# Fewer SBUF operands on VectorE, pinned scaling and builds, and heads contracted in pairs in a two-layer Fourier attention kernel

## The chip, the cores and the metric

One Trainium2 core (float32 throughout). The metric is device time in microseconds (us) of one launch. Lower is better. The kernel before took 567.58, 564.03 and 561.96 us in three runs, median 564.03.

## The reference, cut to what matters

Two layers are applied to x of shape (2, 56, 128, 128): x = x + layer(groupnorm(x)). K, Q, V, P, M0 and M1 are spectral convolutions that keep 32 x 16 modes, each with a 1x1 skip. Below, A = 8 heads.

```python
q, k, v = fno_layer(xa, ...)                 # 1 -> 8 heads for each of 56 channels
scores = einsum('baks,bals->bakl', qh, kh) / sqrt(H * W)
attn = softmax(scores, axis=-1)              # 56 x 56 for each head
out = einsum('bakl,bals->baks', attn, vh)
out = fno_layer(out, Pw, ...)                # 8 heads -> 1
att = inorm(out + xa, gan, ban)
an = inorm(att, g2, b2)
h = fno_layer(an, M0w, ..., norm=True, act=True)      # gelu
h = fno_layer(h, M1w, ..., norm=True)
y = inorm(h, gmo, bmo) + att
```

## The kernel before, in words

The picture is held whole in SBUF (`X2`), and attention is done in the space of modes, where a batch has 56 channels by 32 x 16 complex modes. Each of two layers L works through both batches b. The stages of a batch, with their names in the code, are:

- `turn` (layer 0) or `end` (layer 1) transposes rows on PE (L361) and takes the statistics.
- `modes_chain` finishes the group norm (L454 to L464: tiny operations on 128x1 or 128x2 tiles), scales the plane (L475), transforms it over both axes (L479, L484, L497) to the modes `xf`.
- `gram` and `gram_chain` make the channel matrix (L507, L525) and its norms (`vd` L532).
- `scale_x` multiplies the picture in place by the norm's scale, eight pieces of 120x1024 (L546).
- `scores` (L572, L591), `values` (L613), `softmax_chain` (L630 to L649), `mix_chain` (L657 to L674) and `heads` (L685) are the attention. `AT` is the transposed attention matrix, `MI` the head mixing matrix, `D` the result of `heads`.
- `norms_chain` (L698 to L739) does P, both instance norms and the first inverse transform (`inverse`, L397 and L402).
- `gelu` (L747 to L831) synthesises the picture strip by strip, `h_chain` (L845 to L890) prepares the last one, and `end` (L936, L939) adds everything. In layer 0 POOL's L939 also writes the next layer's picture, which L361 then transposes.

POOL builds the weight matrices `WU`, `WT` and `WM` (`build` L337, `build_m` L344), four instructions each for WU and WT in every layer.

Two things set the order. `_woven(lead, bulk)` traces the steps of a chain of small operations between pieces of bulk work. A scheduler then reorders what it may and writes one list for each engine, and every engine runs its list in order. `tc.keep_in_program_order(i)` forbids the scheduler to move `i` ahead of the instruction traced before it on its engine. PSUM is handed out from two pools: `bank()` has two buffers of one bank, `pair()` three of two banks. An instruction that needs a buffer waits for the last reader of the one it gets.

Of the kernel before, what the change touches and what calls it, by code (L numbers as in the profile page):

```python
# [166 lines left out]
def fno_layers(ctx: ExitStack, tc: tile.TileContext, x, out, weights, small, const):  # L167
# [239 lines left out]
    def multiply(n, src, dst):  # L407
# [12 lines left out]
        S.copy(dst.rearrange("p (h m) -> p h m", h=2), p[:, :, :224])  # L420
# [93 lines left out]
    def gram_chain(L, b, st):  # L514
        xf, p = st["xf"], st["gram"]
        nm = little(f"nm{b}", [1, K])
        V.tensor_scalar(nm, xf[0:1, :K], -float(N * N), None, ALU.mult)
# [14 lines left out]
        V.scalar_tensor_tensor(vd, gc[:, :K], 1.0 / (N * N), ident[:K, :K], ALU.mult, ALU.mult)  # L532
# [21 lines left out]
    def room(b):  # L554
# [7 lines left out]
    def scores(L, b, st):
# [3 lines left out]
        G.tensor_tensor(MI[:K], _bc(ident[:K, :K], 1, HEADS), _bc(d["mix"][:K], 2, K), ALU.mult)  # L566
# [59 lines left out]
    def softmax_chain(L, b, st):  # L626
# [3 lines left out]
        V.tensor_tensor(SC, grid(sc[:, :224], 4), _bc(rl, 1, 4), ALU.mult)  # L630
        top, tot = little(f"top{b}", [N, 4]), little(f"tot{b}", [N, 4])
        V.tensor_reduce(top, SC, AX.X, ALU.max)
        V.tensor_tensor(SC, SC, _bc(top, 2, K), ALU.subtract)
        S.activation(SC, SC, AF.Exp, scale=rk)
        V.tensor_reduce(tot, SC, AX.X, ALU.add)
        V.reciprocal(tot, tot)
        V.tensor_tensor(SC, SC, _bc(tot, 2, K), ALU.mult)
        yield 4.5

        p = pair()  # L640
        for a in range(4):
            for c in range(2):
                for r in range(2):
                    T.matmul(
                        p[64 * r : 64 * r + 64, c, K * a : K * a + K], lhsT=R["SC"][64 * c : 64 * c + K, a, :],
                        rhs=ident[64 * c : 64 * c + K, 64 * c : 64 * c + K], start=True, stop=True,
                        tile_position=(64 * c, 64 * r), skip_group_check=True,
                    )
# [28 lines left out]
    def heads(L, b, st):  # L677
        R = room(b)
        AT, VT = grid(R["AT"]), R["VT"].rearrange("p t (e m) -> p t e m", e=2)
        p = pair()  # L680
        for t in range(4):
            for a in range(HEADS):
                for e in range(2):
                    for c in range(2):
                        T.matmul(  # L685
                            p[64 * e : 64 * e + 64, c, K * t : K * t + K],
                            lhsT=VT[64 * c : 64 * c + K, t, e, 64 * a : 64 * a + 64],
                            rhs=AT[64 * c : 64 * c + K, a, :], start=(a == 0), stop=(a == 7),
                            tile_position=(64 * c, 64 * e), skip_group_check=True,
                        )  # L690
# [4 lines left out]
    def norms_chain(L, b, st):
        (par, d), D, R, pb = prs[L], st["D"], P[b], st["pb"]
        Pm, u, y0, sqy, s1, s2 = (R[:, 448 * j : 448 * j + 448] for j in range(6))
        V.tensor_tensor(Pm, pb[:, :448], D, ALU.add)  # L698
        yield 1.6
        multiply(0, grid(Pm), y0)  # L700
        S.activation(sqy, y0, AF.Square)
        V.scalar_tensor_tensor(u, Pm, 2.0, D, ALU.mult, ALU.subtract)
        V.tensor_tensor(u, u, D, ALU.mult)
# [12 lines left out]
        V.scalar_tensor_tensor(k3[:, 2:3], k3[:, 1:2], EPS, tm, ALU.mult, ALU.add)  # L716
# [7 lines left out]
        v1, v2 = grid(s1), grid(s2)  # L724
# [115 lines left out]
    def h_chain(L, b, st):  # L840
# [7 lines left out]
        V.scalar_tensor_tensor(mv[:, 1:2], mv[:, 0:1], mv[:, 0:1], mv[:, 1:2], ALU.mult, ALU.add)  # L848
# [114 lines left out]
    build(WUv, tcs, 0, range(0, 8, 2))  # L963
# [82 lines left out]
```

## Time and profile before

| | before |
|---|---|
| runs, us | 567.58, 564.03, 561.96 (median 564.03) |
| profiled execution, us | 563.96, of which the span is 562.0 |
| PE (matmul) busy | 465.8 us, 83% of the span |
| DVE (VectorE) busy | 341.3 us, 61% |
| ACT (ScalarE) busy | 191.0 us, 34% |
| POOL (GpSimd) busy | 175.2 us, 31% |
| mean granted TensorE clock | 0.895 of 2.4 GHz |

The span runs from the first to the last instruction. What lies outside it is 1.96 us. A float32 matmul of the program shows as two matmul records in the trace, so x128 there are 64 matmuls of the program. The orders of instructions below count matmuls of the program.

### The profile page before, as it was taken

What the parts mean: (1) busy time and instruction counts of PE and PEld (TensorE: products, weight loads), DVE (VectorE), ACT (ScalarE), POOL (GpSimd) and SP (SyncE); (2) the same over time, 40 slices, a digit from 0 to 9 for tenths busy, and PEclk for the clock granted to TensorE, in tenths of its full rate; (3) what the DMA queues carried; (4) which work ended last, traced back from release to release, by engine and by line L of the source; (5) the groups of instructions that cost most, each with busy time, mean ns of one, the idle gap of its engine ahead of it and who ended that gap; (6) DMA issues with size and microseconds to landing.
All of it is one profiled execution on the core that took longest, in us unless ns stands there. A gap on an engine that the chain in (4) does not pass through costs nothing.

```text
span 562.0 us, 15794 instructions
## 1 busy us (share of the span) xinstructions
PE 465.8 (83%) x7176; PEld 317.9 (57%) x7176; DVE 341.3 (61%) x568; ACT 191.0 (34%) x238; POOL 175.2 (31%) x201
## 2 busy tenths in 40 slices
PE   2347998789989999979659859989989999886695
PEld 2323867659766576636444446958857555543431
DVE  1565387941426885677867977920344874767475
ACT  2432240151437436514213313151546456402000
POOL 2394517991000000055546841910000000055300
PEclk9998896986999998988759969996999998988599
DMA  8991001030000000017443210010000000027434
GB/s 187 240 213 22 2 2 41 6 81 27 3 3 3 1 1 2 1 31 213 150 146 100 69 50 5 7 52 3 3 2 3 1 1 2 1 65 232 132 121 141
DMA packets 13170, 33.29 MB, mean 59 GB/s; under 512 B 2080, under 2 KB 2848, under 8 KB 13088
## 3 DMA queue, kind: packets, MB, share of 16 engines
q1 hardware_dynamic: 12960, 32.23, 21.6%
q8 instruction: 56, 0.92, 0.7%
q10 hardware_dynamic: 144, 0.07, 0.1%
q14 instruction: 10, 0.08, 0.0%
HBM read 21.02 MB, written 11.01 MB: 57 GB/s over the span
## 4 chain that ended last, share of the span: by engine, by line
PE 53%; DVE 21%; ACT 8%; issue 7%; POOL 5%; DMA 5%; DVEq 0%; SPq 0%; POOLq 0%; ACTq 0%
PE pair L762 7%; PE pair L747 6%; PE pair L811 4%; PE pair L591 4%; PE bank L507 4%; PE pair L685 4%; DMA X<-x 3%; PE bank L572 3%; POOL X L939 3%; PE bank L799 2%; DVE WT L402 2%; PE bank L382 2%; PE bank L437 2%; PE bank L327 2%; PE bank L674 2%
## 5 line engine op out<-in xcount | busy, mean ns | idle before, releaser
L369 DVE BATCH_NORM_STATS2 stats<-P 128x6 f32<-128x448 f32 x64 | 35.9, 611 | 43.9 <-ACT P L364 31.9
L831 DVE BATCH_NORM_STATS2 stats<-P 128x6 f32<-128x512 f32 x64 | 40.6, 681 | 18.7 <-ACT P L829 18.6
L546 DVE TENSOR_TENSOR X<-X,gvr 120x1024 f32<-120x1024 f32 x32 | 50.7, 1609 | 0.0
L939 POOL TENSOR_TENSOR X<-P,xr 128x1024 f32<-128x1024 f32 x16 | 38.6, 2427 | 27.6 <-DVE P L936 18.1
L936 DVE SCALAR_TENSOR_TENSOR P<-P,hs,pair 128x1024 f32<-128x1024 f32 x32 | 39.9, 1270 | 11.3 <-PE pair L762 11.0
L829 ACT ACTIVATE P<-pair 128x1024 f32<-128x1024 f32 x32 | 32.6, 1026 | 30.8 <-PE pair L762 30.2
L811 PEld LDWEIGHTS pair<-C,P 120*128 120x128 f32 x256 | 27.7, 147 | 20.6 <-issue 11.5
L747 PE MATMUL pair<-C,WT 32*128 32x128 f32 x512 | 28.3, 325 | 11.8 <-DVE P L936 6.3
L762 PE MATMUL pair<-X,Be 57*64 57x512 f32 x256 | 38.0, 694 | 0.0
L762 PE MATMUL pair<-X,Bs 57*64 57x512 f32 x256 | 37.7, 630 | 0.0
L337 POOL TENSOR_TENSOR WT<-tc,C 128x1024 f32<-128x1024 f32 x8 | 30.0, 3778 | 22.6 <-ACT tc L331 14.6
L507 PE MATMUL bank<-P 128*64 128x56 f32 (+1 forms) x1024 | 36.6, 236 | 0.0
L591 PEld LDWEIGHTS pair<-xf,WU 64*64 64x64 f32 x1024 | 32.8, 136 | 6.5 <-issue 5.7
L811 PE MATMUL pair<-C,P 120*128 120x120 f32 x256 | 35.6, 282 | 0.7 <-ACT P L829 0.5
L747 PEld LDWEIGHTS pair<-C,WT 32*128 32x128 f32 x512 | 23.2, 218 | 22.5 <-issue 8.2
L591 PE MATMUL pair<-xf,WU 64*64 64x56 f32 x1024 | 35.7, 221 | 0.0
L507 PEld LDWEIGHTS bank<-P 128*64 128x64 f32 (+1 forms) x1024 | 34.9, 150 | 0.9 <-issue 0.5
L361 PE MATMUL pair<-C,X 120*128 120x120 f32 x128 | 20.7, 316 | 17.1 <-POOL X L939 17.0
L812 ACT COPY WT<-pair 128x896 f32<-128x896 f32 x32 | 28.9, 906 | 14.3 <-PE pair L811 14.0
L367 ACT COPY P<-pair 128x896 f32<-128x896 f32 x16 | 14.5, 904 | 56.5 <-PE pair L361 56.5
L391 POOL MEMSET WT<- 128x256 f32 x4 | 1.3, 313 | 101.8 <-PE bank L799 68.0
L361 PEld LDWEIGHTS pair<-C,X 120*128 120x128 f32 x128 | 16.5, 167 | 27.7 <-POOL X L939 21.8
(237 smaller groups left out, 877.1 us busy)
## 6 DMA issues: line engine op xcount, KB each, us to landing
X<-x SPq DMA_DIRECT2D x16, 448.0 KB
xr<-x SPq DMA_DIRECT2D x32, 224.0 KB
out<-P SPq DMA_DIRECT2D x32, 224.0 KB
store<-X SPq DMA_DIRECT2D x16, 224.0 KB
xr<-store SPq DMA_DIRECT2D x16, 224.0 KB
stage<-weights SPq DMA_DIRECT2D x2, 544.0 KB
C<-const_all SPq DMA_DIRECT2D x1, 621.0 KB
X<-x SPq DMA_DIRECT2D x2, 256.0 KB
```

The lines of the kernel that those rows point to most:

```text
L361: T.transpose(p[:, s, N * e : N * e + 120], X2[:120, b, i, :], ident[:120, :120])
L369: V.bn_stats(stats[:, 2 * g + s, :], dst[:, 448 * s : 448 * s + 448])
L507: T.matmul(p[u : u + m, :K], lhsT=P[b][:, K * i : K * i + m], rhs=plane[b][:, i, :], start=(i < 2), stop=(i == N - 1), tile_position=(0, u ...
L546: V.tensor_tensor(v, v, _bc(st["gvr"][:120], 1, 8), ALU.mult)
L591: T.matmul(p[64 * e : 64 * e + 64, k, K * a : K * a + K], lhsT=WUv[64 * e : 64 * e + 64, t + k, a, :], rhs=xv[64 * e : 64 * e + 64, t + k, ...
L747: T.matmul(both[j // 2][:, j % 2, N * e : N * e + N], lhsT=Z[32 * j : 32 * j + 32, o : o + N], rhs=C["gw"][32 * j : 32 * j + 32, :], start ...
L762: T.matmul(p[64 * c : 64 * c + 64, r, :], lhsT=Bs[q, :], rhs=X2[q, b, s : s + 4, :].rearrange("p e w -> p (e w)"), start=False, stop=stop, ...
L811: T.transpose(p[:, r, N * e : N * e + 120], h3[:120, o : o + N], ident[:120, :120])
L829: S.activation(h3, both[v].rearrange("p r m -> p (r m)"), AF.Gelu)
L831: V.bn_stats(stats[:, 4 * A + 2 * v + r, :], h3[:, 512 * r : 512 * r + 512])
L936: V.scalar_tensor_tensor(h3, h3, st["hs"], both[v].rearrange("p r m -> p (r m)"), ALU.mult, ALU.add)
L939: G.tensor_tensor(dst, h3, xr[:, n % 3, :], ALU.add)
```

## The change

- **Operands.** VectorE operations on small tiles that read two SBUF tensors become `tensor_scalar` with a column as scalar (L460, L455, L872 and others), or read one operand from PSUM (softmax works on the scores' bank, `multiply` returns its bank, and a `t` in a bank takes one product of L725 and L883). `nm` (L517) and the scaling L885 go to ACT.
- **Heads.** `AT` and `MI` are stored with two heads on the two halves of the partitions, so `mix` takes 4 matmuls in place of 8, the transposes of `AT` 8 in place of 16, and `heads` 64 matmuls of 128 rows in place of 128 of 56. `values` lays out its result to fit: 32 matmuls of 256 columns for 16 of 512.
- **Order.** `scale_x`, `build` and `build_m` are pinned. In the passage to layer 1 the WU builds are traced between the strips of `end` of batch 1. In the diff `G` is POOL, `V` DVE, `S` ACT, `T` PE.

```diff
@@ build
-            G.tensor_tensor(
+            tc.keep_in_program_order(G.tensor_tensor(
...
+            yield
@@ multiply
-        S.copy(dst.rearrange("p (h m) -> p h m", h=2), p[:, :, :224])
+        return p[:, :, :224]
@@ modes_chain
-        V.scalar_tensor_tensor(mv[:, 1:2], mv[:, 0:1], mv[:, 0:1], mv[:, 1:2], ALU.mult, ALU.add)
+        V.tensor_scalar(mv[:, 1:2], mv[:, 0:1], mv[:, 0:1], mv[:, 1:2], ALU.mult, ALU.add)
...
-        V.tensor_tensor(gv, gs[:, 0:1], gs[:, 0:1], ALU.mult)
-        V.tensor_tensor(gv, gs[:, 1:2], gv, ALU.subtract)
-        S.activation(gv, gv, AF.Sqrt, bias=eps)
+        V.tensor_scalar(gv, gs[:, 0:1], gs[:, 0:1], gs[:, 1:2], ALU.mult, ALU.subtract)
+        S.activation(gv, gv, AF.Sqrt, bias=eps, scale=-1.0)
...
-        V.scalar_tensor_tensor(sh, gs[:, 0:1], -1.0, gv, ALU.mult, ALU.mult)
+        V.tensor_scalar(sh, gs[:, 0:1], gv, -1.0, ALU.mult, ALU.mult)
@@ gram_chain
-        V.scalar_tensor_tensor(vd, gc[:, :K], 1.0 / (N * N), ident[:K, :K], ALU.mult, ALU.mult)
+        V.scalar_tensor_tensor(vd, p[:K, :K], 1.0 / (N * N), ident[:K, :K], ALU.mult, ALU.mult)
@@ scale_x
-            V.tensor_tensor(v, v, _bc(st["gvr"][:120], 1, 8), ALU.mult)
+            tc.keep_in_program_order(V.tensor_tensor(v, v, _bc(st["gvr"][:120], 1, 8), ALU.mult))
@@ softmax_chain
-        V.tensor_tensor(SC, grid(sc[:, :224], 4), _bc(rl, 1, 4), ALU.mult)
+        z = grid(sc[:, :224], 4)
+        V.tensor_tensor(z, z, _bc(rl, 1, 4), ALU.mult)
...
-        V.tensor_tensor(SC, SC, _bc(tot, 2, K), ALU.mult)
+        V.tensor_tensor(SC, z, _bc(tot, 2, K), ALU.mult)
@@ heads
-        for t in range(4):
-            for a in range(HEADS):
+        p = bank()
+        for t in range(8):
+            for a in range(4):
                 for e in range(2):
-                    for c in range(2):
-                        T.matmul(
...
+                    T.matmul(
+                        p[64 * e : 64 * e + 64, K * t : K * t + K], lhsT=VT[:, t // 2, e, t % 2, a, :], rhs=AT[:, a, :],
+                        start=(a == 0), stop=(a == 3), tile_position=(0, 64 * e), skip_group_check=True,
+                    )
@@ norms_chain
-        multiply(0, grid(Pm), y0)
-        S.activation(sqy, y0, AF.Square)
...
+        p = multiply(0, grid(Pm))
+        S.activation(halves(sqy), p, AF.Square)
+        V.tensor_copy(halves(y0), p)
...
-        V.tensor_tensor(v1, grid(D), _bc(rows[:, 0, :], 1, 8), ALU.mult)
-        V.tensor_tensor(v2, grid(y0), _bc(rows[:, 1, :], 1, 8), ALU.mult)
-        V.tensor_tensor(s1, s1, s2, ALU.add)
+        t = bank()[:, :448]
+        V.tensor_tensor(grid(t), grid(y0), _bc(rows[:, 1, :], 1, 8), ALU.mult)
+        V.tensor_tensor(grid(s1), grid(D), _bc(rows[:, 0, :], 1, 8), ALU.mult)
+        V.tensor_tensor(s1, s1, t, ALU.add)
@@ h_chain, one line of nine
-        V.tensor_tensor(w_, w_, d["m12"][:K], ALU.mult)
-        V.tensor_tensor(u_, u_, w_, ALU.subtract)
+        V.tensor_scalar(u_, w_, d["m12"][:K], u_, ALU.mult, ALU.subtract)
@@ the passage to layer 1
+            last = end(0, 1, s1, stats[1])
+            next(last)
...
-            build(WUv, tcs, 0, range(0, 8, 2))
-            _run(_woven(modes_chain(1, 0, stats[0], st[1][0]), end(0, 1, s1, stats[1])))
+            _run(_woven(
+                modes_chain(1, 0, stats[0], st[1][0]), _with(last, build(WUv, tcs, 0, range(0, 8, 2))),
+            ))
```

The line numbers of the changed kernel are 2 to 7 higher: L546 becomes L550, L630 L638, L725 and its neighbours L731 to L733, L939 L946, while L337 stays.

First place: DVE in layer 0, before the softmax of batch 0 (L630). `rr` and `vd` belong to `gram_chain`; the tile with the lower number is that of batch 0. Before:

```order
L532 SCALAR_TENSOR_TENSOR vd_843<-gc_840,C 56x56
L546 TENSOR_TENSOR X_86<-X_86,gvr_760 120x1024
L533 TENSOR_REDUCE vc_844<-vd_843 56x1
L546 TENSOR_TENSOR X_86<-X_86,gvr_760 120x1024 x2
L540 RECIPROCAL rr_914<-rr_914 128x57
L546 TENSOR_TENSOR X_86<-X_86,gvr_760 120x1024
L528 COPY gc_994<-bank 56x56
L546 TENSOR_TENSOR X_86<-X_86,gvr_760 120x1024
L532 SCALAR_TENSOR_TENSOR vd_997<-gc_994,C 56x56
L546 TENSOR_TENSOR X_86<-X_86,gvr_760 120x1024
L533 TENSOR_REDUCE vc_998<-vd_997 56x1
L546 TENSOR_TENSOR X_86<-X_86,gvr_760 120x1024
```

In the changed kernel:

```order
L536 SCALAR_TENSOR_TENSOR vd_841<-bank,C 56x56
L537 TENSOR_REDUCE vc_842<-vd_841 56x1
L544 RECIPROCAL rr_912<-rr_912 128x57
L550 TENSOR_TENSOR X_86<-X_86,gvr_553 120x1024
L532 COPY gc_993<-bank 56x56
L536 SCALAR_TENSOR_TENSOR vd_996<-bank,C 56x56
L537 TENSOR_REDUCE vc_997<-vd_996 56x1
L550 TENSOR_TENSOR X_86<-X_86,gvr_553 120x1024 x3
L544 RECIPROCAL rr_1078<-rr_1078 128x57
L550 TENSOR_TENSOR X_86<-X_86,gvr_553 120x1024 x4
L638 TENSOR_TENSOR bank<-bank,rr_912 128x224
L640 TENSOR_REDUCE top_1192<-bank 128x4
```

The scalings between the `vd` lines were those of batch 1 (gvr_760), with batch 0's ahead of the place. They are now batch 0's own, behind its `vd`, and the softmax of batch 0 stands behind all eight. Batch 1's eight stand later, in `norms_chain` of batch 0.

Second place: POOL in the passage from layer 0 to 1. X_86 is the next layer's picture; P_113 is batch 0 and P_114 batch 1. Before:

```order
L939 TENSOR_TENSOR X_86<-P_113,xr 128x1024 x3
L337 TENSOR_TENSOR WU<-tc_1191,C 128x1024 x2
L939 TENSOR_TENSOR X_86<-P_113,xr 128x1024
L566 TENSOR_TENSOR P_113<-C,der_1136 56x448
L337 TENSOR_TENSOR WU<-tc_1191,C 128x1024
L487 COPY P_113<-gv_2969 128x128
L489 TENSOR_SCALAR P_113<-sh_2970 128x1 x2
L939 TENSOR_TENSOR X_86<-P_114,xr 128x1024 x6
L337 TENSOR_TENSOR WT<-tc_1191,C 128x1024 x2
L939 TENSOR_TENSOR X_86<-P_114,xr 128x1024 x2
```

In the changed kernel:

```order
L946 TENSOR_TENSOR X_86<-P_113,xr 128x1024 x4
L572 TENSOR_TENSOR P_113<-C,der_1135 64x224 x2
L491 COPY P_113<-gv_2869 128x128
L493 TENSOR_SCALAR P_113<-sh_2870 128x1 x2
L946 TENSOR_TENSOR X_86<-P_114,xr 128x1024
L337 TENSOR_TENSOR WU<-tc_1190,C 128x1024
L946 TENSOR_TENSOR X_86<-P_114,xr 128x1024
L337 TENSOR_TENSOR WU<-tc_1190,C 128x1024 x2
L946 TENSOR_TENSOR X_86<-P_114,xr 128x1024
L337 TENSOR_TENSOR WU<-tc_1190,C 128x1024
L946 TENSOR_TENSOR X_86<-P_114,xr 128x1024 x3
L337 TENSOR_TENSOR WT<-tc_1190,C 128x1024 x2
```

The WU builds left the adds of batch 0 and stand between those of batch 1. Two WT builds stay ahead of the last two adds of batch 1, which follow the last row.

Third place: DVE in layer 1, where the norms of batch 0 and the softmax of batch 1 meet. P_113 is batch 0's room, P_114 batch 1's. Before:

```order
L725 TENSOR_TENSOR P_113<-D_4002,bank 128x448
L726 TENSOR_TENSOR P_113<-P_113,bank 128x448
L729 TENSOR_TENSOR dc_4066<-bm_4065,bank 1x56
L727 TENSOR_TENSOR P_113<-P_113 128x448
L445 TENSOR_TENSOR Bs_4264<-BTx_3892,bank 128x56
L728 TENSOR_SCALAR P_113<-P_113,C 128x56
L630 TENSOR_TENSOR P_114<-bank,rr_3726 128x4x56
L730 TENSOR_SCALAR P_113<-dc_4066,der_1136 1x56
L632 TENSOR_REDUCE top_4237<-P_114 128x4
```

In the changed kernel:

```order
L550 TENSOR_TENSOR X_86<-X_86,gvr_3320 120x1024 x3
L638 TENSOR_TENSOR bank<-bank,rr_3607 128x224
L640 TENSOR_REDUCE top_4060<-bank 128x4
L641 TENSOR_TENSOR bank<-bank,top_4060 128x224
L643 TENSOR_REDUCE tot_4061<-bank 128x4
L644 RECIPROCAL tot_4061<-tot_4061 128x4
L645 TENSOR_TENSOR P_114<-bank,tot_4061 128x4x56
L731 TENSOR_TENSOR bank<-P_113,bank 128x448
L732 TENSOR_TENSOR P_113<-D_3823,bank 128x448
```

The whole softmax of batch 1, with its bank, now stands ahead of the first product of batch 0's norms, which needs a bank of its own for `t`. Before, the products came first. Layer 0 has the same order.

## Rows read from the trace of the kernel before

**Rows 1.** The page: busy time of the engines (engine, us, share, instructions).

```profile
PE 465.8 (83%) x7176; PEld 317.9 (57%) x7176; DVE 341.3 (61%) x568; ACT 191.0 (34%) x238; POOL 175.2 (31%) x201
```

**Rows 2.** Windows: busy us (count) of PE, PEld, DVE, ACT, POOL; clock, DMA, GB/s.

```profile
90.00:100.00 10.00, 10.00 (x127) 8.37 (x124) 7.47 (x5) 0.18 (x1) 10.00 (x5) 0.54 0.19 57
140.00:240.00 100.00, 96.45 (x1485) 64.92 (x1481) 59.72 (x138) 52.91 (x65) 4.17 (x7) 0.98 0.01 2
...
380.00:390.00 10.00, 9.35 (x202) 8.93 (x206) 0.61 (x3) 0.81 (x3) 0.31 (x1) 0.62 0.01 3
```

**Rows 3.** Waits of PE: line, what it waited for: total us, times, longest.

```profile
PE pair L361 <- POOL X L939: 17.0, 3, 9.4
...
PE bank L479 <- DVE P L475: 8.2, 4, 6.9
...
PE bank L536 <- DVE vd L532: 4.0, 1, 4.0
PE pair L613 <- POOL WT L337: 1.4, 1, 1.4
```

**Rows 4.** Timeline of DVE, 29 to 36 us: start, duration, instruction.

```profile
29.31 3.85 DVE L460 TENSOR_TENSOR gv<-gs 128x1 f32<-128x1 f32 x1
...
34.60 1.60 DVE L475 TENSOR_SCALAR P<-P,gv,sh 128x1792 f32<-128x1792 f32 x1
```

**Rows 5.** Timeline of POOL beside it.

```profile
28.81 0.93 POOL L566 TENSOR_TENSOR P<-C,der 56x448 f32<-56x448 f32 x1
...
33.22 1.33 POOL L273 TENSOR_TENSOR stage<-stage 128x544 f32<-128x544 f32 x1
```

**Rows 6.** Timeline of DVE, `h_chain` of batch 1, both layers.

```profile
262.04 0.14 DVE L867 TENSOR_SCALAR f<-c 56x1 f32<-56x1 f32 x1
...
262.64 2.32 DVE L872 TENSOR_TENSOR f<-f,der 56x1 f32<-56x1 f32 x1
...
279.61 2.03 DVE L885 TENSOR_SCALAR WU<-WU,C 128x56 f32<-128x56 f32 x1
...
509.88 1.87 DVE L858 TENSOR_TENSOR WU<-WU,xf 128x448 f32<-128x448 f32 x1
...
517.49 1.90 DVE L878 TENSOR_TENSOR f<-f,r 56x1 f32<-56x1 f32 x1
```

**Rows 7.** Timeline of POOL beside the first of them.

```profile
261.53 1.06 POOL L344 TENSOR_TENSOR WM<-tc,C 128x512 f32<-128x512 f32 x1
```

**Rows 8.** Lines L546 and L337: count, duration ns minimum/median/maximum, first and last start.

```profile
L546 DVE TENSOR_TENSOR X<-X,gvr x32: 1149/1207/4123, 79.3 to 362.4; 120x1024 f32<-120x1024 f32 x32
...
L337 POOL TENSOR_TENSOR WU<-tc,C x8: 1942/1952/1964, 57.8 to 289.2; 128x1024 f32<-128x1024 f32 x8
L337 POOL TENSOR_TENSOR WT<-tc,C x8: 1944/2922/11702, 87.7 to 353.7; 128x1024 f32<-128x1024 f32 x8
```

**Rows 9.** Timeline of POOL, end of layer 0.

```profile
281.55 2.34 POOL L939 TENSOR_TENSOR X<-P,xr 128x1024 f32<-128x1024 f32 x1
...
317.32 5.82 POOL L337 TENSOR_TENSOR WT<-tc,C 128x1024 f32<-128x1024 f32 x2
327.76 5.66 POOL L939 TENSOR_TENSOR X<-P,xr 128x1024 f32<-128x1024 f32 x2 [4.62 <-DVE P L936]
```

**Rows 10.** Timeline of PE: half of `heads` twice, half of a `gram`.

```profile
103.30 2.07 PE L507 MATMUL bank<-P 128*64 128x56 f32 x64
...
389.05 3.68 PE L685 MATMUL pair<-P 56*64 56x56 f32 x128
...
422.54 2.09 PE L685 MATMUL pair<-P 56*64 56x56 f32 x128
```

**Rows 11.** Timeline of DVE, the third place of the change.

```profile
405.40 0.62 DVE L725 TENSOR_TENSOR P<-D,bank 128x448 f32<-128x448 f32 x1 [3.60 <-PE bank L432]
...
407.61 0.39 DVE L630 TENSOR_TENSOR P<-bank,rr 128x224 f32<-128x224 f32 x1
```

**Rows 12.** Timeline of ACT there.

```profile
405.92 1.28 ACT L634 ACT_TABLE_LOAD   x1
```

More of the change, by code (lines that the diff above doesn't have):

```diff
@@ L405, in inverse, with multiply @@
             )
-    def multiply(n, src, dst):
+    def multiply(n, src):
         p = pair()
@@ L516, in gram_chain @@
         nm = little(f"nm{b}", [1, K])
[L517 removed]
+        S.activation(nm, xf[0:1, :K], AF.Copy, scale=-float(N * N))
         T.matmul(
@@ L565, in scores @@
         G.tensor_tensor(SG[:K], _bc(ident[:K, :K], 1, HEADS), _bc(d["score_g"][:K], 2, K), ALU.mult)
-        G.tensor_tensor(MI[:K], _bc(ident[:K, :K], 1, HEADS), _bc(d["mix"][:K], 2, K), ALU.mult)
+        for c in range(2):
+            q = slice(64 * c, 64 * c + 64)
+            G.tensor_tensor(MI[q], _bc(C["fold"][q, :K], 1, 4), _bc(d["mix"][q, 4 * c : 4 * c + 4], 2, K), ALU.mult)
         G.memset(R["SC"][:, :, K:], 0.0)
@@ L636, in softmax_chain @@
+        V.tensor_tensor(z, z, _bc(top, 2, K), ALU.subtract)
+        S.activation(z, z, AF.Exp, scale=rk)
+        V.tensor_reduce(tot, z, AX.X, ALU.add)
         V.reciprocal(tot, tot)
-        V.tensor_tensor(SC, SC, _bc(tot, 2, K), ALU.mult)
+        V.tensor_tensor(SC, z, _bc(tot, 2, K), ALU.mult)
         yield 4.5
-        p = pair()
+        p = bank()
         for a in range(4):
             for c in range(2):
[L643 to L648, printed above, removed]
@@ L649, in softmax_chain @@
-        S.activation(R["AT"].rearrange("p (c m) -> p c m", c=2), p[:, :, :224], AF.Copy, scale=rk)
-        yield 1.0
+                q = slice(64 * c, 64 * c + K)
+                T.matmul(
+                    p[64 * c : 64 * c + 64, K * a : K * a + K], lhsT=R["SC"][q, a, :], rhs=ident[q, q], start=True, stop=True,
+                    tile_position=(64 * c, 64 * c), skip_group_check=True,
+                )
+        S.activation(R["AT"], p[:, :224], AF.Copy, scale=rk)
+        yield 0.8
     def mix_chain(L, b, st):
@@ L659, in mix_chain @@
+        T.matmul(p[:K, :K], lhsT=ident[:, :K], rhs=ident[:, :K], start=False, stop=True)
         BT = little(f"BT{b}", [K, 64])
@@ L715, in norms_chain @@
         V.tensor_scalar(tm, p[:K, 1:2], d["A02"][:K], None, ALU.mult)
-        V.scalar_tensor_tensor(k3[:, 2:3], k3[:, 1:2], EPS, tm, ALU.mult, ALU.add)
+        V.tensor_scalar(k3[:, 2:3], k3[:, 1:2], EPS, tm, ALU.mult, ALU.add)
         S.activation(k3, k3, AF.Sqrt)
@@ L847, in h_chain @@
         V.bn_aggr(mv, st["stats"].rearrange("p n s -> p (n s)"))
-        V.scalar_tensor_tensor(mv[:, 1:2], mv[:, 0:1], mv[:, 0:1], mv[:, 1:2], ALU.mult, ALU.add)
+        V.tensor_scalar(mv[:, 1:2], mv[:, 0:1], mv[:, 0:1], mv[:, 1:2], ALU.mult, ALU.add)
         V.tensor_scalar(mv, mv, 0.5, None, ALU.mult)
@@ L855, in h_chain @@
         y1, s1, s2 = (fb[:, 448 * j : 448 * j + 448] for j in range(3))
-        multiply(1, grid(hm), y1)
-        S.activation(s1, y1, AF.Square)
-        V.tensor_tensor(s2, y1, hm, ALU.mult)
+        p = multiply(1, grid(hm))
+        S.activation(halves(s1), p, AF.Square)
+        V.tensor_tensor(halves(s2), p, halves(hm), ALU.mult)
+        S.copy(halves(y1), p)
         yield 1.6
@@ L882, in h_chain @@
         rows = spread(*dg)
-        V.tensor_tensor(grid(s2), grid(y1), _bc(rows[:, 0, :], 1, 8), ALU.mult)
-        V.tensor_tensor(s1, s2, D, ALU.add)
-        V.tensor_scalar(s1[:, :K], s1[:, :K], C["syn"], None, ALU.mult)
+        t = bank()[:, :448]
+        V.tensor_tensor(grid(t), grid(y1), _bc(rows[:, 0, :], 1, 8), ALU.mult)
+        V.tensor_tensor(s1, t, D, ALU.add)
+        S.activation(s1[:, :K], s1[:, :K], AF.Copy, scale=C["syn"])
         V.tensor_tensor(s1[0:1, :K], st["dcq"], rows[0:1, 1, :], ALU.subtract)
@@ L962, in fno_layers @@
     ))
-    build(WUv, tcs, 0, range(0, 8, 2))
+    _run(build(WUv, tcs, 0, range(0, 8, 2)))
     for L in range(2):
@@ L967, in fno_layers @@
         _run(_woven(chain(modes_chain(L, 1, stats[1], s1), more), gram(0, s0)))
-        build(WTv, tcs, 16, range(0, 8, 2))
-        build_m(tcs)
+        _run(chain(build(WTv, tcs, 16, range(0, 8, 2)), build_m(tcs)))
         if L == 0:
```

78 lines of the change are left out of this document (36 added, 42 removed).

## The prediction

> **What bounds the kernel now.** Read the busy shares first: PE works 83% of the span and DVE 61% [rows 1]. PE is the bound, but not everywhere, so I split the span into stretches. In 140 to 240 us PE works 96.45 of 100 us at a clock of 0.98 [rows 2]; nothing that helps DVE, ACT or POOL is worth anything there. In other stretches PE stands still, and behind a pause the granted clock sits near its lower level of 1.2 GHz: 0.54 in 90 to 100 and 0.62 in 380 to 390 [rows 2]. A matmul then costs almost twice as much: the same half of `heads` takes 2.09 us or 3.68 [rows 10]. A gap so costs more than its length.
>
> PE's list of waits gives the gaps names: 17.0 us for L939, POOL's adds at the end of layer 0 (9.4 in one), 8.2 for L475, 4.0 for `vd` L532, 1.4 for a WT build [rows 3]. The timelines of DVE and POOL tell why those are late. L460 works on 128 numbers and takes 3.85 us at 29.31 [rows 4], while POOL runs instruction after instruction from 28.81 on; L460 ends at 33.16, and POOL's next long one, L273, starts at 33.22 [rows 5]. In `h_chain` L872 takes 2.32 and L878 1.90, both with two SBUF operands on 56 numbers, where L867 takes 0.14 [rows 6]. POOL is hurt as well: a WU build always takes 1.95, a WT build, which runs beside the scalings L546, up to 11.7 for its time, and a scaling up to 4.12 around a median of 1.21 [rows 8]. **DVE operations with two SBUF operands and POOL hold each other up**, and PE waits behind both.
>
> The Trainium skill, in "SBUF — State Buffer", section "Who interferes with whom", says that a VectorE instruction with two SBUF inputs blocks against a GpSimd instruction that reads SBUF, until the first of the two is done. By that L460 would have waited only for L566, up to 29.74, some 0.4 us; it waited through seven instructions, so the trace is harsher than the page, and the first term below would by the page be 0.4.
>
> **The change, part by part** (+ is time saved, against the profiled execution of 563.96 us, 0.07 below the median; 1.96 of it lies outside the span and stays).
>
> (a) Group norm of batch 0, layer 0. L460 and L461 become one operation with a column as scalar, so up to 3.85 - 0.16 = 3.7 us go. But L475 is next: it took 1.60 at 34.60 while POOL ran [rows 4], and if it now starts inside POOL's run it may be held to the gap at 33.2 [rows 5]. That starts it 1.4 earlier than 34.60. I take **+1.6**; bounds 0.4 and 4.
>
> (b) 66 to 100 us. The early `values` that waited 1.4 for a WT build [rows 3] now stand later, as WT is traced behind. The stretch behind that wait ran at 0.54, so 10 us hold 5.4 of full speed [rows 2], and 4.6 were lost. I take 1.4 and half of 4.6: **+3.5**; bounds 0 (another wait sends the clock down) and 6.
>
> (c) Scalings. They leave the place ahead of `vd`, so PE's 4.0 wait for it [rows 3] goes. In exchange all eight of batch 0, 8 x 1.21 = 9.7 us [rows 8], stand ahead of its softmax, which delays it a little: I take 1.2. Net 2.8 in layer 0, and 1 in layer 1, where no such wait is listed: **+3.8**; bounds -1 and 6.
>
> (d) Two heads at once. `heads` goes from 128 matmuls to 64, but the old ones use four quarters of the array and the new ones two halves. 64 old ones take 2.09, 33 ns each; L507 has the new form (128 rows, two column halves, 56 columns), and 32 of those take 2.07, 65 ns each [rows 10]. So 128 x 33 = 4.2 becomes 64 x 65 = 4.1: nothing. What is left is 8 fewer transposes at 33 and 4 fewer mix matmuls at 65, half a microsecond, four times: **+2**; bounds 0 and 4.
>
> (e) Norms of batch 0 beside the softmax of batch 1. Now the products start at 405.40 and the softmax at 407.61 [rows 11]. In the new order the whole softmax stands first, since `t` wants a bank. It can't start before the scores end, at 407.6. Its six short DVE and ACT operations of 0.39 [rows 11] make 2.4, and the load of ACT's table, 1.28 and so far hidden behind a wait [rows 12], now waits for DVE and joins the chain: the products start at about 411.3, 6 us late. PE's list has the transposes of AT, the inverse and then `values` in that order, so PE can't run past. Two pinned scalings of 1.21 also precede the transposes L402. Some 0.5 is won back, as part of the scores is earlier: 5.5, and 1 for more time at the low clock. Twice: **-13**; bounds -6 and -22.
>
> (f) End of layer 0. From 283.9, when batch 0's last add ends, to the last of batch 1, 333.4, is 49.5 us [rows 9]. POOL's work in it will be eight adds of 2.34 [rows 9], four WU and two WT builds of 1.95 [rows 8]: 30.4, since no scaling runs beside it; and batch 0's last add comes up to 3.9 earlier, two WU builds being gone from ahead of it. What PE can get is its 17.0 of waiting [rows 3]. DVE's and DMA's part stays, and two WT builds still stand ahead of the last adds (2 x 1.95 in place of 5.82 [rows 9]). I take **+13**, `h_chain`'s gains in layer 0 included; bounds 4 (the two WU builds alone) and 18 (with the clock).
>
> (g) `h_chain` of batch 1, layer 1. L878 loses 1.75 and L858 1.2 [rows 6]; the pieces that read `multiply` and `t` from PSUM about 1 more: **+4**; bounds 1 and 5. Elsewhere the same edits lie under PE's work [rows 2] and count nothing; if PE were not full there, each would give some tenths.
>
> Sum: 1.6 + 3.5 + 3.8 + 2 - 13 + 13 + 4 = 14.9, so 563.96 - 14.9 = **549 us**.
>
> **The rivals.**
>
> *Slower: the scalings sit in the softmax's way.* Batch 1's eight pinned scalings (9.7 us, [rows 8]) all stand in DVE's list inside the norms of batch 0. I hid all but 2.4 of them in waits. If they don't fit, inverse, AT and mix come up to 9.7 later per layer, PE pauses, and `heads` of batch 1 runs at 3.68 per half instead of 2.09, 3.2 more [rows 10]. That is 6.5 + 9.7 + 3.2 = 19.4 per layer, 38.8 in place of 13: 575 us. It decides for slower when (e) costs over 33.5. For it: the clock did fall after such a pause at 380 [rows 2]. Against it: DVE has an idle 3.60 just there, ahead of L725 [rows 11]. Chance 0.13.
>
> *No change: the stall only changes its owner.* A `tensor_scalar` may be held by POOL too. For it: L885 took 2.03 on 128x56 with one tensor operand in SBUF [rows 6]. Against it: L867, a `tensor_scalar` on 56 numbers, took 0.14 while POOL's L344 ran from 261.53 to 262.59 [rows 6, 7]. Then (a) is 0.4, (b) and (c) 1 each, (g) 0.5, and (f) 9: 0.4 + 1 + 1 + 2 - 13 + 9 + 0.5 = 0.9, or 563 us. Chance 0.15. The Trainium skill, same page and section, says that `tensor_scalar` can enter a mode that takes the port shared with GpSimd, which is this rival's rule; L885 agrees, L867 doesn't.
>
> *More: (e) costs nothing,* because PE has batch 0's synthesis to do meanwhile. Against it: in PE's list just six of those matmuls stand ahead of the mix of batch 1. Then 549 - 13 = 536 us. Chance 0.11.
>
> *More: two heads at once do halve `heads`.* If 128 rows cost 33 ns like 56 rows, 2 us go four times: 541 us. L507 speaks against it [rows 10]. Chance 0.06.
>
> **How the numbers follow.** The forecast has 0.55, with a range of its own of 541 to 558 from the bounds; 549 is its middle. The range goes from the third rival to the second, 536 to 564, and leaves out the first. One per cent, 5.6 us, is what can be told from no change here. Faster by more: 0.52 of the forecast, 0.17 of the third and fourth, 0.02 of the second: 0.71. Within: 0.03 and 0.13 of the forecast and the second, 0.16. Slower: 0.13, the first.
>
> **What will show it.** (a) gv's operation takes 0.16, and L479's wait at 36 shrinks by less than 2. (c) no wait for `vd`; scalings behind it with a median near 1.2 and no maximum over 2. (d) half of the new `heads` takes 2.1 at full clock, not 1.05. (e) a wait for the inverse's input, and the ACT table load between two steps of softmax 1. (f) WT builds of about 2, L361's 9.4 gone, adds of batch 1 done 31 to 40 us after those of batch 0. (g) L878's successor at 0.15. I am wrong if (e) is hidden or doubled, or if L361 still waits for POOL: those two terms are the largest and of opposite sign.

## The result and the profile after

The changed kernel took 553.75 us (median of four runs) against 563.8: a ratio of 0.967, 95% interval 0.956 to 0.978. A second series gave 556.03 against 565.1, 0.983 (0.978 to 0.988). Both lie in the forecast range, 5 to 7 us above the forecast of 549. Its runs spread from 543.28 us at a mean granted clock of 0.927 to 561.92 at 0.896. The ratios here and below leave out, for both kernels, the runs that took over 1.5% longer than the fastest of the same kernel in the same series, so they differ from the quotient of the medians (553.75/563.8 = 0.982). The profiled execution, 547.76 us with a span of 546.0, is one of the shorter ones.

The busy shares of the changed kernel, to be held against [rows 1]: PE is busy 7 us less, DVE 23, POOL 17.

```profile
PE 458.8 (84%) x6696; PEld 315.0 (58%) x6696; DVE 318.6 (58%) x556; ACT 190.3 (35%) x242; POOL 158.5 (29%) x205
```

PE's waits, against [rows 3]. The waits of L540 for `vd` (L536) and of the early `values` for a WT build no longer appear:

```profile
PE pair L363 <- POOL X L946: 13.4, 10, 3.0
...
PE bank L652 <- DVE Bs L450: 10.6, 2, 5.3
...
PE bank L483 <- DVE P L479: 2.4, 3, 2.0
```

The 9.4 us wait for one add is gone, the wait for the scaled plane shrank from 8.2 to 2.4, and 10.6 us of a new wait came. The scalings and the WT builds, against [rows 8]: no scaling takes over 2.1, and every WT build takes 1.95.

```profile
L550 DVE TENSOR_TENSOR X<-X,gvr x32: 1160/1214/2052, 93.4 to 390.9; 120x1024 f32<-120x1024 f32 x32
...
L337 POOL TENSOR_TENSOR WT<-tc,C x8: 1944/1950/1955, 81.2 to 333.8; 128x1024 f32<-128x1024 f32 x8
```

Time follows best by landmarks, here the starts and ends of groups on PE's timeline, in us of the span. "+ t" is the changed kernel with one edit, told below, in its second trace.

| landmark | before | changed | its 2nd trace | two heads alone | two heads + pin | changed + t |
|---|---|---|---|---|---|---|
| layer 0: first gram | 57.4 | 51.9 | 56.0 | 52.4 | 52.3 | 55.2 |
| last gram ends | 105.4 | 94.6 | 98.5 | 100.1 | 99.8 | 97.3 |
| heads 0, start to end | 125.3-136.4 | 111.5-119.2 | 115.6-123.1 | 119.2-126.2 | 114.5-126.6 | 114.4-126.9 |
| heads 1 starts | 161.7 | 150.6 | 154.4 | 150.4 | 153.7 | 153.8 |
| inverse of batch 1 | 185.6 | 178.8 | 182.6 | 174.4 | 177.7 | 178.5 |
| layer 1: first transposition | 250.0 | 242.8 | 249.1 | 241.5 | 241.7 | 242.8 |
| last transposition | 335.5 | 315.8 | 322.5 | 324.1 | 319.0 | 317.2 |
| heads 0, start to end | 381.5-392.7 | 361.7-368.8 | 368.7-375.7 | 368.6-377.0 | 364.8-371.9 | 363.1-370.2 |
| heads 1 starts | 418.0 | 400.1 | 407.1 | 401.2 | 397.1 | 395.5 |
| inverse of batch 1 | 441.9 | 428.3 | 435.2 | 428.0 | 421.1 | 420.2 |
| last matmul ends | 555.9 | 539.9 | 547.0 | 541.2 | 532.9 | 531.4 |

The changed kernel's lead over before runs 5.5, 10.8, 17.2, 11.1, 6.8, 7.2, 19.7, 23.9, 17.9, 13.6, 16.0. It falls twice by 10 us, in the same place of both layers, and what the passage to layer 1 wins, 12.5, comes in one piece.

### The profile page after: what moved, and what is told of

The parts are those of the page before. It is cut to its first block, busy times and chain, and to the rows that moved or that the text cites. A ratio compares the mean times of both kernels' runs of the same rounds, so it can differ in the third digit from the quotient of the medians.

```text
span 546.0 us, 14842 instructions
## 1 busy us (share of the span) xinstructions
PE 458.8 (84%) x6696; PEld 315.0 (58%) x6696; DVE 318.6 (58%) x556; ACT 190.3 (35%) x242; POOL 158.5 (29%) x205
## 4 chain that ended last, share of the span: by engine, by line
PE 53%; DVE 20%; POOL 7%; DMA 7%; ACT 6%; issue 5%; SPq 1%; DVEq 0%; POOLq 0%; ACTq 0%
PE pair L768 8%; PE pair L753 6%; PE pair L817 5%; POOL X L946 5%; PE pair L597 5%; PE bank L511 5%; PE bank L691 3%; DMA X<-x 3%; PE bank L805 3%; DMA xr<-x 3%; DVE WT L404 2%; DVE X L550 2%; PE bank L578 2%; PE bank L442 2%; PE bank L327 2%
## 5 line engine op out<-in xcount | busy, mean ns | idle before, releaser
L943 DVE SCALAR_TENSOR_TENSOR P<-P,hs,pair 128x1024 f32<-128x1024 f32 x32 | 40.1, 1270 | 12.7 <-PE pair L768 12.5
L946 POOL TENSOR_TENSOR X<-P,xr 128x1024 f32<-128x1024 f32 x16 | 37.5, 2355 | 19.4 <-DMA xr<-x 11.2
L817 PEld LDWEIGHTS pair<-C,P 120*128 120x128 f32 x256 | 29.0, 152 | 21.2 <-issue 8.5
L550 DVE TENSOR_TENSOR X<-X,gvr 120x1024 f32<-120x1024 f32 x32 | 40.3, 1303 | 0.0
L768 PE MATMUL pair<-X,Bs 57*64 57x512 f32 x256 | 40.2, 671 | 0.0
L817 PE MATMUL pair<-C,P 120*128 120x120 f32 x256 | 36.8, 291 | 0.5 <-DVE P L404 0.5
L818 ACT COPY WT<-pair 128x896 f32<-128x896 f32 x32 | 28.9, 906 | 14.0 <-PE pair L817 12.5
L753 PE MATMUL pair<-C,WT 32*128 32x128 f32 x512 | 24.1, 294 | 9.1 <-DVE WT L404 4.4
L753 PEld LDWEIGHTS pair<-C,WT 32*128 32x128 f32 x512 | 19.4, 189 | 20.5 <-issue 12.0
L361 PE MATMUL pair<-C,X 56*128 56x56 f32 x256 | 16.7, 282 | 16.4 <-DMA X<-x 10.7
L363 PE MATMUL pair<-C,X 120*128 120x120 f32 x128 | 18.8, 297 | 13.4 <-POOL X L946 13.4
L363 PEld LDWEIGHTS pair<-C,X 120*128 120x128 f32 x128 | 14.9, 155 | 23.3 <-POOL X L946 20.0
```

The lines of the kernel that those rows point to most:

```text
L363: T.transpose(p[:, s, N * e : N * e + 120], X2[:120, b, i, :], ident[:120, :120])
L550: tc.keep_in_program_order(V.tensor_tensor(v, v, _bc(st["gvr"][:120], 1, 8), ALU.mult))
L753: T.matmul(both[j // 2][:, j % 2, N * e : N * e + N], lhsT=Z[32 * j : 32 * j + 32, o : o + N], rhs=C["gw"][32 * j : 32 * j + 32, :], start ...
L768: T.matmul(p[64 * c : 64 * c + 64, r, :], lhsT=Bs[q, :], rhs=X2[q, b, s : s + 4, :].rearrange("p e w -> p (e w)"), start=False, stop=stop, ...
L817: T.transpose(p[:, r, N * e : N * e + 120], h3[:120, o : o + N], ident[:120, :120])
L943: V.scalar_tensor_tensor(h3, h3, st["hs"], both[v].rearrange("p r m -> p (r m)"), ALU.mult, ALU.add)
```

## The experiments

All were timed beside runs of the kernel before; ratios are to those, with 95% intervals. The landmarks of the text are read as in the table.

**1. The group norm's small operations alone**, on the kernel before:

```diff
-        V.tensor_tensor(gv, gs[:, 0:1], gs[:, 0:1], ALU.mult)
-        V.tensor_tensor(gv, gs[:, 1:2], gv, ALU.subtract)
+        V.tensor_scalar(gv, gs[:, 0:1], gs[:, 0:1], gs[:, 1:2], ALU.mult, ALU.subtract)
...
```

> The kernel before with the group norm's edits alone (three VectorE operations of two SBUF operands become tensor_scalar with a column). Theory: in the changed kernel the first gram of layer 0 starts at 51.9 us instead of 57.4, and these edits alone do that: gram at 52 to 53, L460's successor at 0.16, the wait of PE for L475 6.9 us shorter by at least 3; time 558 to 561 if the lead is kept. Rival: the stall only moves to L475 (the 128x1792 scaling), which is then held by POOL: gram at 55 to 56 and time 562 to 564.

561.74 us, 0.995 (0.990 to 0.999). DVE and then POOL in this kernel (start, duration, instruction):

```profile
29.22 0.27 DVE L460 TENSOR_SCALAR gv<-gs 128x1 f32<-128x1 f32 x1
...
30.30 3.67 DVE L474 TENSOR_SCALAR P<-P,gv,sh 128x1792 f32<-128x1792 f32 x1
```
```profile
31.70 1.32 POOL L272 TENSOR_TENSOR stage<-stage,C 128x544 f32<-128x544 f32 x1
33.10 2.07 POOL L273 TENSOR_TENSOR stage<-stage 128x544 f32<-128x544 f32 x1
```

The rival's mechanism was right: L460 takes 0.27, and the plane's scaling L474 (L475 in the kernel before) is held past the end of POOL's L272 at 33.02. The matmuls behind it start 2.2 us earlier (34.13 for 36.35). The first gram starts just 0.2 earlier (57.2), later than either expectation, since the clock fell to 0.50 between 45 and 46 us here and at 48 in the kernel before.

**2. Two heads at once alone**, on the kernel before: `values`, AT, the mixing matrix, `mix` and `heads` as in the change.

> The kernel before with two heads contracted at once (values, AT, mixing matrix, mix and heads of the changed kernel) and nothing else. Theory: the new form gains through the clock. In four kernels with the old form the heads of batch 0 took 11.1 to 12.0 us in 8 of 8 cases, in six with the new form 7.0 to 9.0 in 10 of 12; so here 7.0 to 7.7 in batch 0 of both layers, 2 x 4 + 2 = 10 us in all, 554 to 556. Rival 1: it is worth only the matmuls saved, 2 us, and heads of batch 0 stays above 11: 562 to 564. Rival 2: AT in a single bank now waits for the banks of the norms, which takes 5 us per layer back: 560 or more with fast heads.

549.6 us, 0.975 (0.968 to 0.981): 15 us from this part alone, no less than the 10 and 9 us of the whole change by its medians, and more than was expected. Windows around the heads of batch 0, layer 0, in the kernel before, in this one, and in that of experiment 3 (columns as in [rows 2]); the last is the kernel before again, around the heads of batch 1:

```profile
125.30:136.40 11.10, 11.10 (x287) 10.71 (x287) 0.43 (x3) 0.21 (x1) 2.83 (x12) 0.55 0.22 60
```
```profile
119.20:126.20 7.00, 7.00 (x155) 6.57 (x154) 0.43 (x3) 0.21 (x1) 3.58 (x15) 1.00 0.47 118
```
```profile
118.50:130.40 11.90, 11.90 (x284) 11.47 (x284) 0.43 (x3) 0.21 (x1) 4.64 (x18) 0.50 0.17 48
```
```profile
161.70:168.40 6.70, 6.70 (x286) 6.39 (x284) 0.43 (x3) 0.21 (x1) 0.41 (x2) 1.00 0.02 5
```

PE works all the time in each, but in batch 0 the old form ran at 0.55 and 0.50 of the clock and the new one at 1.00. In batch 1 the old form ran at 1.00 too. At full clock half of the new `heads` takes what the old took:

```profile
124.12 2.08 PE L686 MATMUL bank<-P 128*64 128x56 f32 x64
```

So what the heads gain isn't in the matmuls but in the level of the clock. By the table, this kernel ends 14.7 us ahead. 6.9 of them come within the two heads of batch 0 (4.1 and 2.8), 4.5 in the stretches just ahead of and behind these heads, and 5.0 have been there since the first gram; the other stretches together take 1.7 back. Those 5.0 are the surprise, and they are no gain of `heads`: L460 still reads two SBUF operands here.

```profile
29.57 0.53 DVE L460 TENSOR_TENSOR gv<-gs 128x1 f32<-128x1 f32 x1
...
31.08 1.41 DVE L475 TENSOR_SCALAR P<-P,gv,sh 128x1792 f32<-128x1792 f32 x1
```
```profile
29.51 0.56 POOL L568 TENSOR_TENSOR P<-C,der 64x224 f32<-64x224 f32 x1
...
30.97 0.56 POOL L568 TENSOR_TENSOR P<-C,der 64x224 f32<-64x224 f32 x1
31.61 2.08 POOL L271 TENSOR_TENSOR stage<-stage,C 128x544 f32<-128x544 f32 x1
```

The mixing matrix is now built by two short POOL instructions. One ends at 30.07, and L460 ends at 30.10; then it is POOL's L271 that is held, 2.08 for 1.32. The matmuls behind the scaling start at 32.63, 3.7 us earlier than in the kernel before; the other 1.3 of the 5.0 go with the moment at which the clock fell, which varies (experiment 12).

**3. The opposite**: the changed kernel with one head at a time.

> The changed kernel with values, AT, mixing matrix, mix and heads as before (one head at a time, four quarters of the array). Theory: heads gains nothing from two heads at once, since 64 records take 2.08 us in the new form and 128 records 2.09 in the old one at full clock; the transposes and the mix give about half a us a time, so 2 us in all: the same within 1 per cent. Rival: fewer matmuls are a real gain of 8 us or more, and the time rises to 556 or above. The transposes of AT use a pair of banks here, so they may also wait less for a bank, worth up to 5 us the other way.

566.51 us, 1.000 (0.996 to 1.004): without the pairs the rest of the change is worth nothing. Heads took 11.9, 6.6, 11.2 and 10.8 (in its longest run, 576.98 us, which is the one profiled). PE's wait of 10.6 for a bank is gone here, as AT takes a pair, but the inverse waits 13.1 for the norms (L399 for L736). Over all traces of this study, heads of batch 0 took 11.1 us or more in 8 of 8 cases in the old form. In the new form 5 of 20 took 12 to 12.5, and the others 7.0 to 9.0. All 5 stand in layer 0 with pinned scalings, where they are 5 of 8. In batch 1 the old form took 6.6 to 6.7 in 5 of 8 cases, so the form alone doesn't set the level.

**4. The pin alone**, on the kernel before:

```diff
-            V.tensor_tensor(v, v, _bc(st["gvr"][:120], 1, 8), ALU.mult)
+            tc.keep_in_program_order(V.tensor_tensor(v, v, _bc(st["gvr"][:120], 1, 8), ALU.mult))
```

> The kernel before with the scalings of the picture pinned and nothing else. Theory: most of the gain at the end of layer 0 and the wait for vd come from the scalings no longer running beside POOL: PE's 4.0 us wait for vd gone, WT builds at a median near 2 us instead of 2.9, PE's wait for POOL's adds 17.0 falls to 8 or less, time about 563.9 - 3 - 8 = 553. Rival: the weight builds' place makes that gain: the wait for the adds stays at 14 or more, and the time is 559 to 562. The norms of batch 0 keep their place ahead of the softmax of batch 1 here, so the mix of batch 1 should not be late.

565.86 us, 1.005 (1.000 to 1.010), for 553 expected. The mechanism is there, the time isn't. PE's wait for the adds fell from 17.0 to:

```profile
PE pair L361 <- POOL X L939: 10.3, 3, 6.7
```

and layer 1's transpositions take 75.6 us from first to last, not 85.5. But the heads took 12.0, 8.2, 11.9 and 10.8 (before: 11.1, 6.7, 11.2, 6.6), 7.3 us back at the low clock.

**5. The change without the pin**

> The changed kernel with the scalings not pinned (the scheduler puts them early again, beside POOL's builds and adds). Theory: the pin is what makes the end of layer 0 shorter (75.6 us from the first to the last transposition in the kernel before with the pin alone, 85.5 without, 73.0 in the changed kernel): here 80 to 86 again, scalings with a maximum over 4 us, and PE waits 4 us for vd; 553 to 560. Rival: the edits on the operands and the place of the builds suffice, and it stays at 544 to 552; the norms of batch 0 would even gain 2.4 us a layer, as no scaling stands ahead of L404.

572.84 us, 1.013 (1.008 to 1.018), the slowest of all and beyond both expectations. The transpositions take 82.7 us, scalings up to 4.1 us, and two waits are back:

```profile
PE pair L363 <- POOL X L946: 18.6, 9, 7.6
...
PE bank L540 <- DVE vd L536: 4.7, 2, 4.2
```

**6. Two heads and the pin together**, on the kernel before, without any edit on operands, builds or the passage:

> The kernel before with two heads at once and the scalings pinned, and none of the edits on operands, builds or the passage. Theory: these two parts are nearly all of it. Two heads at once gave 549.6 us; the pin took 9.9 us out of the passage to layer 1 (85.5 to 75.6) and nothing shows it lost but heads at the low clock, which the new form avoids: 549.6 - 10 to 13 = 537 to 540, as t in SBUF here too leaves the products ahead of the softmax of batch 1 (537 for the changed kernel with t in SBUF). Rival: the edits on the operands are worth 5 us or more by themselves, and the time is 543 or above.

540.83 us, 0.964 (0.957 to 0.970), a little above the expected 537 to 540. That is 13 and 15 us below the medians of the changed kernel. Its ratio is clear of that kernel's second series (0.978 to 0.988), but not of the first (0.956 to 0.978). So two parts of the change are worth as much as the whole, and probably more.

**7. The product t back in SBUF**, one line of the changed kernel:

```diff
-        t = bank()[:, :448]
+        t = R[:, 2240:2688]
```

> The changed kernel with one edit: the product t in the norms of batch 0 goes to SBUF as before, so it wants no PSUM bank. Theory: the lack of a bank is why the softmax of batch 1 stands ahead of the products and why the transposes of AT wait 5.3 us in each layer; without it the products come first, PE's wait at L652 for L450 (10.6 us) goes, the mix of batch 1 is 6 to 7 us earlier in each layer, and the drop of the clock 14 us behind that pause (1.65 us instead of 0.98 for L442, 4 us in each layer) goes too: 547.8 - 2 x 7 - 2 x 4 = 526 us. Rival 1: the pause only moves to the softmax, with the mix of batch 1 at most 2 us earlier: 544 to 548. Rival 2: the pause goes but the clock drops anyway: 534.

537.23 us, 0.952 (0.944 to 0.961): 17 and 19 us below the medians of the changed kernel. By the ratios the gap is some 8 us to its first series, with overlapping intervals, and 17 to the second. What it removes is seen on the changed kernel's PE, at the third place of the change:

```profile
139.85 0.86 PE L652 MATMUL bank<-C,P 56*64 56x56 f32 x10 [5.29 <-DVE Bs L450]
140.64 3.25 PE L399 MATMUL pair<-P,C 64*128 64x224 f32 x16
```

AT waits 5.3 us for a bank that the norms hold, and the inverse then runs at the low clock (3.25; 1.78 otherwise). Some 25 us later, with PE working again and the heads of batch 1 done at full speed, the clock falls once more to 0.50 for some 7 us, in both layers, and the lead shrinks by 4.3 there in each:

```profile
161.24 0.99 PE L442 MATMUL bank<-C,P 128*56 128x1 f32 x16
...
164.59 1.65 PE L442 MATMUL bank<-C,P 128*56 128x1 f32 x16
```

With t in SBUF both are gone in layer 0: 162 to 177 us ran at 1.00. In layer 1 a fall came (0.80 from 403 to 420); the second trace has none there. Whether the wait for the bank causes the second fall is not shown. Between the heads and the inverse of batch 1 the clock fell in 7 of the 8 layers of the four traces in which AT waits for that bank (the exception is layer 0 of experiment 10), and in 4 of 12 with the new `heads` and no such wait, both layers of experiment 9 among them. 526 was expected, too low: the heads of batch 0 in layer 0 took 12.5 in this kernel.

**8. The same once more**

> The changed kernel with t in SBUF once more, for more times beside the others: 533 to 541 again. Heads of batch 0 in layer 0, 12.5 us at the low clock in its first trace, should take 7.5 or 12.5 again, by chance.

536.65 us, 0.946 (0.940 to 0.953), and 12.5 us for those heads again.

**9. Scalings of batch 1 moved** into the gelu of batch 0, besides t in SBUF:

```diff
-            norms_chain(L, 0, s0), _with(scores(L, 1, s1), scale_x(1, s1)),
+            norms_chain(L, 0, s0), scores(L, 1, s1),
...
-        _run(_woven(chain(norms_chain(L, 1, s1), more), gelu(L, 0, s0)))
+        _run(_woven(chain(norms_chain(L, 1, s1), more), _with(gelu(L, 0, s0), scale_x(1, s1))))
```

> The changed kernel with t in SBUF (537.2 us) and, besides, the eight scalings of batch 1 moved from the norms of batch 0 to the gelu of batch 0, where PE is busy all the time. Theory: DVE's list is free of 9.7 us of scalings in the stage that PE waits in, and L404 and the softmax of batch 1 come 2.4 us earlier: the mix of batch 1 another 2 us earlier in each layer, 530 to 534. Rival: the scalings there sat in DVE's waits already, or they now delay the norms of batch 1: 536 to 540.

547.71 us, 0.965 (0.959 to 0.971), 11 us worse than without it and beyond both expectations. The norms of batch 1 come late behind the scalings: from `multiply` to the inverse of batch 1 took 22.3 us in each layer against 16.0 and 18.7 in the first trace of experiment 7, and PE waits for it. Part of the 22.3 is a fall of the clock to 0.50 for some 6 us in that stretch.

```profile
PE pair L399 <- DVE P L736: 4.1, 2, 2.0
```

**10. The old passage to layer 1**, in the changed kernel: the WU builds traced before the end of batch 1.

> The changed kernel with the WU builds of layer 1 traced ahead of the end of batch 1, as before, so that three of them stand ahead of batch 0's last adds or of batch 1's first. Theory: their place costs what the pinning doesn't: PE's wait for the adds rises from 13.4 to 17 to 19 us and the time by 3 to 6, to 551 to 554. Rival: only the scalings' place mattered, and the time stays at 547 to 548.

550.8 us (544.9 to 556.1), 0.969 (0.958 to 0.981): not told apart from the changed kernel, and not slower. PE's wait for the adds fell to 6.4, where 17 to 19 were expected, and its transpositions take 70.1 us against 73.0 and 73.4.

**11. Both, t in SBUF and the old passage**

> The changed kernel with t in SBUF and the WU builds of layer 1 traced ahead of batch 1's end, as before. Theory: the new place costs a little, since from the first to the last transposition of layer 1 it took 73.0 and 73.4 us with it and 70.1 without: 3 us less than t_in_sbuf, 533 to 536. Rival: the clock made that difference, and the time is that of t_in_sbuf within 2 us.

534.32 us, 0.940 (0.933 to 0.947), the best version: by the medians 5% below the kernel before (564.54) and 3.5 to 4% below the changed kernel. Against experiment 8 (536.65) the passage isn't told apart by the times; the transpositions take 69.4 for 74.4.

**12. The changed kernel again**

> The changed kernel once more, for a second trace and more times. Theory: the granted clock falls at moments that the program doesn't fix, so that the same instructions cost several us more or less in the same stretch: the first gram of layer 0 (51.9 us in the first trace, 54.9 and 55.7 in two other traces whose code is the same up to there) lies between 51 and 57 again, and times spread over 543 to 562. Rival: 547.8 is what this kernel takes, and the gram stands at 52 again.

556.03 us. The first gram stood at 56.0. Up to there this kernel shares its code with the changed one's first trace (51.9) and those of 5, 7, 8, 9, 10 and 11 (55.2, 54.9, 55.2, 56.2, 55.7, 55.3). The clock's fall between 40 and 60 us comes at another moment each time: in the first trace it stayed at 1.00 from 38 to 51 us, in this one it went to 0.50 between 41 and 42. So 547.8 isn't what this kernel takes each time, and the rival was wrong.

## Why the prediction was right in sum, and where not

The forecast of 549 lies 5 to 7 us off, with the direction right, but two of its terms were wrong by 5 us and more, with opposite signs. By the landmarks of the first trace, (d) brought 7.5 us in place of 2 (what the lead grows within the two heads of batch 0), and (e) cost 20.7 in place of 13 (what it loses from their ends to the inverse of batch 1). That the sum came out close is in part luck.

**(a) Group norm.** Expected 1.6; experiment 1 gives 2.2 by the mechanism named, the stall moving to L475. In the changed kernel the matmuls start 4.0 earlier (32.30 for 36.35), and PE's wait for the plane shrinks from 6.9 to 2.0, where less than 2 was named as the sign, since L479 isn't held:

```profile
29.86 0.27 DVE L465 TENSOR_SCALAR gv<-gs 128x1 f32<-128x1 f32 x1
...
30.94 1.21 DVE L479 TENSOR_SCALAR P<-P,gv,sh 128x1792 f32<-128x1792 f32 x1
```

The difference is POOL's shorter mixing-matrix instructions, which shift its long ones by 2 us. I had costed that edit at nothing, though without any edit on the operands it gives 3.7 (experiment 2); the two gains overlap and don't add. The lead of 5.5 at the first gram holds the clock's moment besides: it is 1.4 in the second trace.

**(b), (c).** From the first to the last gram of layer 0 the lead grows by 5.3 (5.5 in the second trace); 3.5 was expected. From the last gram to the heads: 19.9 before, 16.9 and 17.1 after (2.8 or 3.0; 2.8 expected). In layer 1, 46.0 became 45.9 (1 expected). Without the pin those stretches are 22.4 and 49.5.

**(d) Two heads at once is the step that failed.** "So 128 x 33 = 4.2 becomes 64 x 65 = 4.1: nothing. What is left is ... half a microsecond, four times: +2". The row was right, 64 records do take 2.08. But I priced both forms at full clock, though the last window of [rows 2] (0.62 in 380 to 390) and [rows 10] (3.68) showed the old form at about half of it in layer 1. Experiments 2 and 3 measure 15 us for this part on the kernel before, of which 5 stand ahead of the first gram, and 10.5 within the changed one (566.51 against 556.03). The fourth rival had the size of this term, 8 us more, with the wrong mechanism.

**(e) The norms of batch 0** held as named: softmax first, then the products (137.90), and the table load inside the chain (ACT's L642, 1.28 at 135.09). PE waits there for the norms' bank. From the end of heads 0 to the start of heads 1 the lead shrinks by 6.1 and 6.0, for 6.5 forecast. Missing was the second fall of the clock behind it, 4.3 more a layer: 13 forecast, 20.7 by the landmarks, and 17 to 19 by the medians of experiments 7 and 8 (553.75 and 556.03 against 537.23 and 536.65).

**(f) The passage.** 85.5 us became 73.0, 12.5 of the 13 forecast. The cause is another than I gave half of it to: the pin alone makes 9.9, and the new place of the WU builds nothing, or costs 3 us. Nor did the gain come out of the 17.0 us of waiting as I had it. L363 still waits 13.4 us for POOL (8.9 in the second trace), which I had named as a sign of being wrong, and batch 1's last add ends 43.5 us behind batch 0's, for 31 to 40 forecast (the last adds of either batch):

```profile
268.91 2.34 POOL L946 TENSOR_TENSOR X<-P,xr 128x1024 f32<-128x1024 f32 x1 [2.99 <-DMA xr<-x]
...
310.08 4.66 POOL L946 TENSOR_TENSOR X<-P,xr 128x1024 f32<-128x1024 f32 x2
```

In the windows of the passage, before and after, PE is idle 6.7 us less in all and busy 5.8 less, at a clock of 0.88 for 0.76:

```profile
249.99:335.47 85.48, 62.58 (x606) 39.23 (x604) 67.05 (x86) 21.90 (x27) 52.29 (x27) 0.76 0.43 124
```
```profile
242.79:315.84 73.05, 56.83 (x590) 34.01 (x592) 48.62 (x77) 22.44 (x29) 50.94 (x29) 0.88 0.52 146
```

**(g)** Expected 4, about 2 seen (2.4 and 2.2 by the last landmarks). L878's successor takes 0.21, and the stall moved on to the diagonal, two instructions behind it:

```profile
503.64 0.21 DVE L884 TENSOR_SCALAR f<-f,r 56x1 f32<-56x1 f32 x1
...
503.90 1.63 DVE L432 TENSOR_SCALAR dg<-C,f,sm 56x56 f32<-56x56 f32 x1
```

So of the rivals, "the stall only changes its owner" is true in places (L475 in experiment 1, the diagonal here), and "the scalings sit in the softmax's way" isn't: in layer 0 DVE stood idle for 2.34 us ahead of that softmax, and the bank was what PE waited for. **Not settled:** why the old form of `heads` stayed at the low clock in batch 0. PE is busy without a gap in both forms. The longest pause of PE just ahead of those heads was 2.64 us in the changed kernel's layer 0 and 1.40 in the kernel before. And the same code has come out both ways. The heads of batch 0 in layer 0, in the changed kernel and in experiment 8, whose edit comes later in the code:

```profile
111.50:119.20 7.70, 7.70 (x153) 7.20 (x151) 0.43 (x3) 0.30 (x2) 4.83 (x19) 0.91 0.35 87
```
```profile
114.40:126.90 12.50, 12.50 (x153) 11.72 (x151) 0.43 (x3) 0.25 (x2) 4.60 (x18) 0.50 0.00 1
```

The rows (56 or 128), the quarters or halves of the array and the buffer (a pair or one bank) changed together and weren't tried apart.

## What to carry to other kernels

Price a matmul at the clock of the stretch that it stands in, and look whether another form of the same work runs at another level; here that made 7.0 and 8.4 us out of 11.1 and 11.2 in two stretches of experiment 2. An intermediate in PSUM spares VectorE an SBUF operand and costs a buffer: with two banks, one more tile put a whole softmax ahead of a chain that PE waited for, and one line gave 17 us of the medians back. When a stalled instruction is given a form that isn't held, look at the next one on its engine that is. And trace a kernel more than once: two traces of the changed one end 7.1 us apart.

## What was not expected of the hardware

L460, with both operands in SBUF, took 3.85 us behind seven POOL instructions in the kernel before, and 0.53 in experiment 2, where it ended with the one POOL instruction that it met. POOL's list shows no gap at either of the two ends (the next instruction starts at 29.73 behind an end at 29.74, and at 30.05 behind 30.07), so why it got through there and not in the kernel before is open. A `tensor_scalar` of 128x1792 took 3.67, 1.60, 1.41 or 1.21 in the same place of four kernels, by what POOL did beside it; where it got through, POOL's instruction was held instead (2.08 for 1.32). And the first gram started between 51.9 and 56.2 us in eight traces with the same code up to there, by the moment at which the granted clock went to 1.2 GHz.
